# Counting degrees by row over 64 node numbers, scatters behind their piece, four piece buffers, gathers in pairs

## The chip, the core and the metric

The kernel runs on one core of one Trainium2 chip. The metric is the device time of one execution in microseconds, the median of three runs. A profiled execution of the same program gives the trace that all lines below come from. PE is TensorE, ACT is ScalarE, DVE is VectorE, POOL is GpSimd and SP is SyncE.

## The reference, cut to what matters

A graph transformer of two layers over N = 6250 nodes and E = 100000 edges. The edges come sorted by destination. Nodes have one of 16 types, edges one of 32.

```python
def gt_layer(x, ntype, etype, src, dst, Wk, Wq, Wv, Wa, Watt, Wmsg, pri, skip, g, b):
    k = typed_linear(x, ntype, Wk).reshape(n, H, HS)      # and q, v alike
    kT = jnp.einsum('nhd,htdo->nhto', k, Watt)
    vT = jnp.einsum('nhd,htdo->nhto', v, Wmsg)
    kw = kT[src, :, etype]
    m = vT[src, :, etype]
    a = jnp.einsum('ehd,ehd->eh', kw, q[dst]) * pri[:, etype].T / SQRT_D
    att = edge_softmax(a, dst, n)
    msg = (m * att[:, :, None]).reshape(-1, H * HS)
    hag = jax.ops.segment_sum(msg, dst, num_segments=n)
    h = jax.nn.silu(typed_linear(hag, ntype, Wa))
    h = h * alpha + x * (1.0 - alpha)
    return (h - mu) * jax.lax.rsqrt(var + 1e-05) * g + b
```

Two such layers, a last linear layer, and a layer norm over x plus the result. D = 128, H = 8 heads of HS = 16.

## The kernel before

For each layer the kernel first makes a table in HBM, `tabs[l]`: for every node and every edge type the row of 256 numbers kT and vT. The edges of a node then need only gathers: one row of the table per edge. Nodes are sorted by their degree within classes of types, so that the nodes of a block of 128 have nearly the same number of edges; there are NB = 50 such blocks.

The part before the first edge gather, up to `prep.close()`, has these pieces of work:

- **Load and test.** The edges' destinations lie in `dsti`, 128 rows of EC = 782 edges (the last row padded with node number N). L441 to L448 count how often a destination is smaller than the one before. If that is ever so, `tc.If(unsorted > 0)` (L497) sorts the edges by a loop of 782 rounds; otherwise the branch is skipped.
- **Table of layer 0.** Nodes are placed by type (`inv`, `rows1`). For every type t the generator `linears0` (L844) gathers x rows (`xg`, L852), transposes them and makes kT and vT of the type's window. `table_block` (L279) then makes, for each block of 128 nodes, two *pieces* `st` (128 x 4096 f32, 2 MB): for each of the two halves kT and vT of a piece it runs matmuls into PSUM (`tb`, L291) for four pairs of heads and copies them to `st` on ACT (L298), or, for the pairs in `share`, on DVE (L296). It yields after each half. A finished piece goes to HBM by one indirect scatter on POOL (`put0`, L898). `st` has STB0 = 3 buffers. There are 98 pieces.
- **Ranking beside it.** `rank_order` (L566) is a generator whose steps are interleaved with the halves by the loop at L907 to L931. It first runs `degrees` (L450): 46 chunks of 17 edges per row, for each chunk two comparisons on DVE that make one-hot matrices of the destination's low 7 bits (`ol`, L465) and high bits (`oh`, L468), and 17 matmuls (L472) that add them up to the number of edges of each node. Then come the node order (histogram L591 and L600, ranks L696 to L707, and `say`, L735 to L747, which carries node data to rank order as `meta`), and last the rank's gathers: for each of 13 groups of up to four blocks, the edge lists `ell` (L778), the x rows in rank order `xr` (L787), and the store of these rows `xrd` (L790). The yields say "degrees", "gathers", "done", or nothing.
- **The loop.** `stage` is the last word that was yielded. `share` is empty while stage is "" or "degrees", else (1,): one pair of four goes to DVE. After each half the ranking moves on by two steps, in the gathers by one step per piece (on the odd half). A finished piece is kept in `late`; it is scattered when the next piece is made, or later.

POOL's instructions stand in the order in which the program writes them (`manual_schedule`); the other engines' are put in order by a scheduler at build time. After `prep.close()` a load of `over` picks the arm; the `fast` arm runs the edge gathers (L1143) of both layers.

Of the kernel before, what the change touches and what calls it, by code (L numbers as in the profile page):

```python
# [9 lines left out]
F32 = mybir.dt.float32  # L10
BF16 = mybir.dt.bfloat16
I32 = mybir.dt.int32
# [101 lines left out]
def kernel(  # L114
# [44 lines left out]
    STB0 = 3  # L159
# [283 lines left out]
    nfalls = pp.tile([P, 1], F32, name="nfalls")  # L443
    nc.vector.tensor_reduce(nfalls, falls, axis=AX.X, op=ALU.add)
    nf_ps = pps.tile([1, 1], F32, name="ps")
    nc.tensor.matmul(nf_ps, nfalls, ones[:, 0:1], start=True, stop=True)
    nfi = pp.tile([1, 1], I32, name="nfi")
    nc.vector.tensor_copy(nfi, nf_ps)  # L448

    def degrees(got):  # L450

        loi = pp.tile([P, EC], I32, name="loi", tag="lo")
        hii = pp.tile([P, EC], I32, name="hii", tag="srci")
        lob = pp.tile([P, EC], BF16, name="lob")
        hib = pp.tile([P, EC], BF16, name="hib")
        nc.vector.tensor_single_scalar(loi, dsti, P - 1, op=ALU.bitwise_and)
        nc.vector.tensor_single_scalar(hii, dsti, 7, op=ALU.arith_shift_right)
        nc.vector.tensor_copy(lob, loi)
        nc.vector.tensor_copy(hib, hii)
        deg_ps = pps.tile([P, NT], F32, name="ps")  # L460
        for c in range(NCH):
            cols = slice(c * J, (c + 1) * J)
            ol = pp2.tile([P, J, P], BF16, name="ol")
            oh = pp2.tile([P, J, NT], BF16, name="oh")
            nc.vector.tensor_tensor(ol, lob[:, cols].unsqueeze(2).to_broadcast([P, J, P]),  # L465
                                    colb.unsqueeze(1).to_broadcast([P, J, P]), op=ALU.is_equal)
            yield "degrees"
            nc.vector.tensor_tensor(oh, hib[:, cols].unsqueeze(2).to_broadcast([P, J, NT]),  # L468
                                    colb[:, :NT].unsqueeze(1).to_broadcast([P, J, NT]),
                                    op=ALU.is_equal)  # L470
            for j in range(J):
                nc.tensor.matmul(deg_ps, ol[:, j, :], oh[:, j, :],  # L472
                                 start=(c == 0 and j == 0), stop=(c == NCH - 1 and j == J - 1))
            yield "degrees"
        yield
        deg = pp.tile([P, NT], F32, name="deg")
        nc.vector.tensor_copy(deg, deg_ps)
# [14 lines left out]

    unsorted = nc.values_load(nfi[0:1, 0:1], min_val=0, max_val=P * EC)
# [3 lines left out]
    with tc.If(unsorted > 0):  # L497
        found = []
        for _ in degrees(found):
            pass  # L500
# [46 lines left out]
        both = pp.tile([P, EC, 2], I32, name="both")  # L547
# [16 lines left out]
    with tc.manual_schedule(engines={mybir.EngineType.Pool}):  # L564

        def rank_order():  # L566
# [208 lines left out]

            for i0, k in superblocks(NB):
# [7 lines left out]
                yield "gathers"  # L784
# [5 lines left out]
                nc.gpsimd.dma_start(rows(xrd, i0, k), xr[:, :k])  # L790
                yield "gathers"
            yield "done"

            onehot = pp.tile([P, NB, TY], F32, name="onehot", tag="both")
# [760 lines left out]
```

## Time and profile before

| what | us |
|---|---|
| median of three runs (3449.41 to 3453.79) | 3449.84 |
| the profiled execution | 3441.72 |
| its span, first to last instruction | 3439.9 |
| first edge gather (L1143) issued at | 803.08 |
| first piece copied (L298) at, end of the sorted branch (L456) at | 57.38, 42.62 |
| PE, PEld, DVE, ACT, POOL busy over the span | 1804.8, 859.6, 2061.4, 996.2, 2207.3 |
| L1143, 1734 gathers, busy | 1703.1 |
| L898, 98 scatters, busy up to 860 us | 156.2 |

The profile page names an engine, a line of the kernel, the tiles written and read, the number of instructions, the busy time and the mean of one; after it the idle time of the engine just before these instructions, and what ended it. Up to 803 us the waits that matter are those around the pieces:

```profile
POOL tab L898 <- ACT st L298: 223.2, 58, 15.7
ACT st L298 <- PE tb L291: 193.2, 128, 5.5
...
ACT st L298 <- DMA tab<-st,rows: 168.9, 48, 16.0
DVE st L296 <- DMA tab<-st,rows: 150.5, 44, 9.0
```

Each line tells who waited for whom, the total in us, how often, and the longest. A wait of ACT or DVE for "DMA tab<-st,rows" is one for a free buffer: the scatter that reads it has not finished.

### The profile page before, as it was taken

How to read it: one execution, taken by the hardware profiler on the slowest of the kernel's cores; microseconds unless marked ns; L12 is line 12 of the kernel's file. 1: busy time of each engine (PE TensorE's matmuls, PEld its weight loads, DVE VectorE, ACT ScalarE, POOL GpSimd, SP SyncE). 2: the span in 40 equal slices, each digit the busy share in tenths (PEclk: the TensorE clock that was granted, in tenths of full speed). 3: DMA queues.
4: the chain of work that ended last, by engine and by line, in shares of the span. 5: the costliest groups of instructions: out<-in, count | busy, mean ns of one | idle time of the engine just before them, and what ended most of it. 6: DMA issues, size and time to landing. Idle time of an engine off the chain costs nothing. (4 is left out here: it accounts for less than half of the span.)

```text
span 3439.9 us, 24065 instructions
## 1 busy us (share of the span) xinstructions
PE 1804.8 (52%) x6428; PEld 859.6 (25%) x6428; DVE 2061.4 (60%) x4345; ACT 996.2 (29%) x1634; POOL 2207.3 (64%) x2213
## 2 busy tenths in 40 slices
PE   4779776893067667777778777601112122121313
PEld 2445333451022232333233222201001111011111
DVE  8967511223566676667667765346656666566765
ACT  2543333561025223432344246301111111021111
POOL 3741366325767777678777776177767777777773
PEclk9768755666577776877787887655555555555555
DMA  6576476898348656775788488733433333343331
GB/s 173 244 300 272 186 264 261 360 423 246 104 156 282 215 197 233 284 262 196 239 290 294 168 301 324 295 107 114 110 98 109 111 112 106 112 116 110 111 105 50
DMA packets 194493, 691.24 MB, mean 201 GB/s; under 512 B 55469, under 2 KB 106032, under 8 KB 169298
## 3 DMA queue, kind: packets, MB, share of 16 engines
q0 software_dynamic: 119120, 651.15, 53.8%
q1 hardware_dynamic: 58838, 31.29, 3.4%
q10 hardware_dynamic: 16384, 7.11, 1.0%
q8 instruction: 55, 0.90, 0.1%
q14 instruction: 96, 0.79, 0.1%
HBM read 264.91 MB, written 429.48 MB: 202 GB/s over the span
## 5 line engine op out<-in xcount | busy, mean ns | idle before, releaser
L1143 POOL DMA_INDIRECT kv<-tab,ell x1734 | 1703.1, 982 | 573.4 <-issue 460.3
L298 ACT COPY st<-tb 128x512 f32<-128x512 f32 (+1 forms) x1024 | 704.4, 759 | 589.7 <-PE tb L291 335.4
L276 PE MATMUL nb<-ident,hag 128*128 128x128 f32 x100 | 26.1, 399 | 758.4 <-DVE hag L1193 758.4
L1155 DVE TENSOR_TENSOR kv<-kv,tb 128x512 f32<-128x512 f32 (+3 forms) x234 | 150.7, 646 | 379.2 <-DMA kv<-tab,ell 370.5
L1155 DVE TENSOR_TENSOR kv<-kv,q 128x512 f32<-128x512 f32 (+3 forms) x234 | 151.8, 651 | 357.3 <-DMA kv<-tab,ell 346.7
L291 PE MATMUL tb<-bdv,vT 32*128 32x512 f32 x784 | 308.0, 912 | 99.4 <-ACT st L298 97.7
L898 POOL DMA_INDIRECT tab<-st,rows x98 | 156.2, 1594 | 276.6 <-ACT st L298 223.2
L291 PE MATMUL tb<-bdv,kvT 32*128 32x512 f32 x800 | 266.9, 790 | 69.6 <-ACT st L298 69.2
L1159 DVE TENSOR_REDUCE a<-kv 128x32 f32<-128x512 f32 (+3 forms) x468 | 298.2, 640 | 2.2
L296 DVE COPY st<-tb 128x512 f32<-128x512 f32 (+1 forms) x160 | 116.6, 730 | 291.5 <-DMA tab<-st,rows 150.5
L291 PE MATMUL tb<-bdk,kT 32*128 32x512 f32 x784 | 260.2, 938 | 3.3 <-DVE st L296 3.3
L270 PE MATMUL nb<-xm,wa 128*128 128x384 f32 (+1 forms) x384 | 209.7, 708 | 86.6 <-DVE xm L261 86.3
L291 PE MATMUL tb<-bdk,kvT 32*128 32x512 f32 x800 | 241.5, 780 | 19.5 <-ACT st L298 19.0
L1354 POOL DMA_INDIRECT tab<-st,row x100 | 114.8, 1148 | 148.7 <-ACT st L298 104.6
L276 PEld LDWEIGHTS nb<-ident,hag 128*128 128x128 f32 x100 | 15.6, 197 | 778.0 <-issue 560.3
L261 DVE SCALAR_TENSOR_TENSOR xm<-ntb,nb 128x384 f32<-128x384 bf16 (+1 forms) x336 | 185.6, 593 | 38.1 <-PE nb L276 23.7
L270 PE MATMUL nb<-xm,wq 128*128 128x384 f32 (+1 forms) x192 | 100.5, 685 | 139.1 <-DVE xm L261 138.9
L291 PEld LDWEIGHTS tb<-bdv,vT 32*128 32x128 f32 x784 | 107.9, 253 | 189.6 <-ACT st L298 168.5
L1045 ACT COPY tb<-q 128x128 f32<-128x128 f32 x50 | 13.4, 269 | 469.8 <-DVE sums L1088 347.1
L1288 PE MATMUL nb<-xm,wkqv 128*128 128x384 f32 (+1 forms) x288 | 126.3, 590 | 38.4 <-DVE xm L261 28.0
L270 PEld LDWEIGHTS nb<-xm,wa 128*128 128x128 f32 x384 | 94.9, 260 | 200.1 <-DVE xm L261 117.8
L1307 PE MATMUL nb<-xm,wkqv 128*128 128x384 f32 (+1 forms) x288 | 132.5, 619 | 15.1 <-DVE xm L261 14.7
(289 smaller groups left out, 2958.1 us busy)
## 6 DMA issues: line engine op xcount, KB each, us to landing
kv<-tab,ell POOLq DMA_INDIRECT x1734
hr<-xrd SPq DMA_DIRECT2D x30, 192.0 KB, 3.2
hr<-xrd SPq DMA_DIRECT2D x15, 256.0 KB, 4.5
xrd<-xr POOLq DMA_DIRECT2D x11, 256.0 KB
ntb<-typed SPq DMA_DIRECT2D x20, 96.0 KB, 7.2
hrd<-hs SPq DMA_DIRECT2D x10, 192.0 KB, 3.7
qrd<-q SPq DMA_DIRECT2D x10, 192.0 KB, 3.2
q<-qrd SPq DMA_DIRECT2D x10, 192.0 KB, 3.3
```

What stands on the lines that cost most here:

```text
L261: nc.vector.scalar_tensor_tensor(xm[:, :n], ntb[:, :n], float(t), hT[:, :n], op0=ALU.is_equal, op1=ALU.mult)
L270: nc.tensor.matmul(ps[:, :n], w[:, t, :], xm[:, :n], start=(t == types[0]), stop=(t == types[-1]))
L291: nc.tensor.matmul(pt[:, b], yT[s, i * P:(i + 1) * P], bd[s, tt, :], start=True, stop=True)
L296: nc.vector.tensor_copy(to, pt)
L298: nc.scalar.copy(to, pt)
L898: put = nc.gpsimd.indirect_dma_start(out=tabs[0].rearrange("(n t) c -> n (t c)", t=16), out_offset=bass.IndirectOffsetOnAxis(ap=rows1[:, t ...
L1143: get = nc.gpsimd.indirect_dma_start(out=kv[:, j - j0, :], out_offset=None, in_=tabs[l][:], in_offset=bass.IndirectOffsetOnAxis(ap=ell[:, ...
L1155: nc.vector.tensor_tensor(kk, kk, q.unsqueeze(1).to_broadcast([P, c, D]), op=ALU.mult)
L1159: nc.vector.tensor_reduce(a[:, j0:j1, :], kk.rearrange("p k (h d) -> p k h d", h=H), axis=AX.X, op=ALU.add)
L1288: nc.tensor.matmul(outs[j][:, :n], wkqv[:, j, t, :], xm[:, :n], start=(t == types[0]), stop=(t == types[-1]))
L1307: nc.tensor.matmul(ps[:, :n], wkqv[:, j, t, :], xm[:, :n], start=(t == types[0]), stop=(t == types[-1]))
L1354: put = nc.gpsimd.indirect_dma_start(out=tabs[1].rearrange("(n t) c -> n (t c)", t=16), out_offset=bass.IndirectOffsetOnAxis(ap=row2[:, tg ...
```

## The change

Four things are changed in the part before the first edge gather.

1. **Degrees by row.** A row of sorted edges holds few node numbers in succession. The new `degrees` takes the lowest number of each row and counts, for each of the NEAR = 64 numbers from there on, how many of the row's 782 edges have it: one `tensor_scalar` with an accumulated column per number. 16 groups of four numbers then go through one-hot matrices (f32) and a matmul each to the nodes. `nfalls` is also set where a row's numbers span 64 or more; then the branch of L497 is taken, which counts with the old code (now `degrees_any`). The part after the counts is a function of its own, `ordered`. Degrees now yield nothing instead of "degrees", and less often.
2. **Scatters.** `store` issues the scatter at once; `late` is gone. `st` has four buffers. `both`, `lob`, `hib`, `ol` and `oh` of the branch share other tiles' room.
3. **Rank gathers in pairs.** `ell` and `xr` gathers yield after two, and the `xrd` store of a group is issued after the `ell` gathers of the next.
4. **Steps.** One ranking step per half, not two. DVE shares copies in the gathers and after them, and before that in every second block only.

```diff
@@ -156,7 +156,8 @@
     KO = [sum(KB[:b]) for b in range(NB)]
     KS = sum(KB)
     PAD = P * EC + P
-    STB0 = 3
+    STB0 = 4
+    NEAR = 64
     assert D == P and H * HS == D and H == 8 and HS == 16 and EC % J == 0 and NP > N and L == 2
     assert max(KB) * H + P <= 512 and max(KB) <= P and min(KB) >= CH and NR >= NP and NB <= P and TY == NC * TC
 
@@ -440,41 +441,24 @@
     falls = pp.tile([P, EC], F32, name="falls", tag="lo")
     nc.vector.tensor_tensor(falls[:, :EC - 1], dsti[:, :EC - 1], dsti[:, 1:], op=ALU.is_gt)
     nc.vector.tensor_tensor(falls[:, EC - 1:], dsti[:, EC - 1:], nxt, op=ALU.is_gt)
-    nfalls = pp.tile([P, 1], F32, name="nfalls")
-    nc.vector.tensor_reduce(nfalls, falls, axis=AX.X, op=ALU.add)
-    nf_ps = pps.tile([1, 1], F32, name="ps")
-    nc.tensor.matmul(nf_ps, nfalls, ones[:, 0:1], start=True, stop=True)
+    nfalls = pp.tile([P, 2], F32, name="nfalls")
+    nc.vector.tensor_reduce(nfalls[:, 0:1], falls, axis=AX.X, op=ALU.add)
+    lowest = pp.tile([P, 1], F32, name="lowest")
+    nc.vector.tensor_copy(lowest, dsti[:, 0:1])
+    nc.vector.tensor_scalar(nfalls[:, 1:2], dsti[:, EC - 1:], lowest, None, op0=ALU.subtract)
+    nc.vector.tensor_scalar(nfalls[:, 1:2], nfalls[:, 1:2], float(NEAR), None, op0=ALU.is_ge)
+    nc.vector.tensor_tensor(nfalls[:, 0:1], nfalls[:, 0:1], nfalls[:, 1:2], op=ALU.max)
+    nf_ps = pps.tile([P, 1], F32, name="ps")
+    nc.tensor.matmul(nf_ps, ones, nfalls[:, 0:1], start=True, stop=True)
     nfi = pp.tile([1, 1], I32, name="nfi")
-    nc.vector.tensor_copy(nfi, nf_ps)
-
-    def degrees(got):
-
...
-        deg_ps = pps.tile([P, NT], F32, name="ps")
-        for c in range(NCH):
-            cols = slice(c * J, (c + 1) * J)
-            ol = pp2.tile([P, J, P], BF16, name="ol")
-            oh = pp2.tile([P, J, NT], BF16, name="oh")
-            nc.vector.tensor_tensor(ol, lob[:, cols].unsqueeze(2).to_broadcast([P, J, P]),
-                                    colb.unsqueeze(1).to_broadcast([P, J, P]), op=ALU.is_equal)
-            yield "degrees"
-            nc.vector.tensor_tensor(oh, hib[:, cols].unsqueeze(2).to_broadcast([P, J, NT]),
-                                    colb[:, :NT].unsqueeze(1).to_broadcast([P, J, NT]),
-                                    op=ALU.is_equal)
-            for j in range(J):
-                nc.tensor.matmul(deg_ps, ol[:, j, :], oh[:, j, :],
-                                 start=(c == 0 and j == 0), stop=(c == NCH - 1 and j == J - 1))
-            yield "degrees"
-        yield
-        deg = pp.tile([P, NT], F32, name="deg")
-        nc.vector.tensor_copy(deg, deg_ps)
+    nc.vector.tensor_copy(nfi, nf_ps[0:1, :])
+    far = pp.tile([P, 1], F32, name="far")
+    nc.vector.tensor_scalar(far, nf_ps, 1.0, None, op0=ALU.min)
+    deg_far = pp.tile([P, NT], F32, name="deg_far")
+    nc.vector.memset(deg_far, 0.0)
+
+    def ordered(got, deg):
+
         tot_ps = pps.tile([P, NT], F32, name="ps")
         nc.tensor.matmul(tot_ps, ones, deg, start=True, stop=True)
         tot = pp.tile([P, NT], F32, name="tot")
@@ -490,13 +474,81 @@
         got.append((deg, ptr))
         yield
 
+    def degrees_any(got):
...
+        nc.vector.tensor_copy(deg_far, deg_ps)
+        yield from ordered(got, deg_far)
+
+    def degrees(got):
+
+        rel = pp.tile([P, EC], F32, name="rel", tag="lo")
+        nc.vector.tensor_scalar(rel, dsti, lowest, None, op0=ALU.subtract)
+        nid = pp.tile([P, NEAR], I32, name="nid")
+        nc.vector.tensor_scalar(nid, colf[:, :NEAR], lowest, None, op0=ALU.add)
+        parts = pp.tile([P, 2, NEAR], I32, name="nidparts")
+        nc.vector.tensor_single_scalar(parts[:, 0], nid, P - 1, op=ALU.bitwise_and)
+        nc.vector.tensor_single_scalar(parts[:, 1], nid, 7, op=ALU.arith_shift_right)
+        at = pp.tile([P, 2, NEAR], F32, name="nidat")
+        nc.vector.tensor_copy(at, parts)
+        yield
+        near = pp.tile([P, NEAR], F32, name="near")
+        same = pp.tile([P, EC], BF16, name="same_dst", tag="eti")
+        deg_ps = pps.tile([P, NT], F32, name="ps")
+        for c0 in range(0, NEAR, SB):
+            for c in range(c0, c0 + SB):
+                nc.vector.tensor_scalar(same, rel, float(c), None, op0=ALU.is_equal, op1=ALU.add,
+                                        accum_out=near[:, c:c + 1])
+            yield
+            sl = slice(c0, c0 + SB)
+            ol = pp2.tile([P, SB, P], F32, name="oc")
+            nc.vector.tensor_tensor(ol, at[:, 0, sl].unsqueeze(2).to_broadcast([P, SB, P]),
+                                    colf.unsqueeze(1).to_broadcast([P, SB, P]), op=ALU.is_equal)
+            oh = pp2.tile([P, SB, NT], F32, name="rh", bufs=1)
+            nc.vector.tensor_tensor(oh, at[:, 1, sl].unsqueeze(2).to_broadcast([P, SB, NT]),
+                                    colf[:, :NT].unsqueeze(1).to_broadcast([P, SB, NT]),
+                                    op=ALU.is_equal)
+            nc.vector.tensor_tensor(oh, oh, near[:, sl].unsqueeze(2).to_broadcast([P, SB, NT]),
+                                    op=ALU.mult)
+            for c in range(c0, c0 + SB):
+                nc.tensor.matmul(deg_ps, ol[:, c - c0, :], oh[:, c - c0, :],
+                                 start=(c == 0), stop=(c == NEAR - 1))
+            if c0 % 8:
+                yield
+        yield
+        deg = pp.tile([P, NT], F32, name="deg")
+        nc.vector.tensor_copy(deg, deg_ps)
+        nc.vector.tensor_tensor(deg_far, deg_far, deg, op=ALU.subtract)
+        nc.vector.scalar_tensor_tensor(deg, deg_far, far, deg, op0=ALU.mult, op1=ALU.add)
+        yield from ordered(got, deg)
+
     unsorted = nc.values_load(nfi[0:1, 0:1], min_val=0, max_val=P * EC)
 
     cnt = dram.tile([NP + P, 1], I32, name="cnt")
     order = dram.tile([P * EC, 2], I32, name="order")
     with tc.If(unsorted > 0):
         found = []
-        for _ in degrees(found):
+        for _ in degrees_any(found):
             pass
         ptr = found[0][1]
         ptri = pp.tile([P, NT], I32, name="ptri")
@@ -544,7 +596,7 @@
             nc.gpsimd.indirect_dma_start(
                 out=order[:], out_offset=bass.IndirectOffsetOnAxis(ap=pos[:, 0:1], axis=0),
                 in_=pair, in_offset=None)
-        both = pp.tile([P, EC, 2], I32, name="both")
+        both = tp.tile([P, EC, 2], I32, name="both", tag="st", bufs=STB0)
         nc.sync.dma_start(both, order.rearrange("(p j) c -> p j c", p=P))
         nc.vector.tensor_copy(dsti, both[:, :, 0])
         nc.vector.tensor_copy(kvi, both[:, :, 1])
@@ -773,6 +825,7 @@
             nc.sync.dma_start(typed, tyr)
             yield "gathers"
 
+            stored = []
             for i0, k in superblocks(NB):
                 for b in range(i0, i0 + k):
                     nc.gpsimd.indirect_dma_start(
@@ -781,17 +834,22 @@
 
                     nc.vector.tensor_scalar(neg[:, KO[b]:KO[b] + KB[b]], colf[:, :KB[b]],
                                             degr[:, b:b + 1], -BIG, op0=ALU.is_ge, op1=ALU.mult)
-                yield "gathers"
+                    if (b - i0) % 2 or b == i0 + k - 1:
+                        yield "gathers"
+                if stored:
+                    nc.gpsimd.dma_start(*stored.pop())
                 xr = tp.tile([P, SB, D], F32, name="xr")
                 for i in range(k):
                     nc.gpsimd.indirect_dma_start(
                         out=xr[:, i, :], out_offset=None, in_=x,
                         in_offset=bass.IndirectOffsetOnAxis(ap=some[:, i0 + i:i0 + i + 1], axis=0))
-                nc.gpsimd.dma_start(rows(xrd, i0, k), xr[:, :k])
-                yield "gathers"
+                    if i % 2 or i == k - 1:
+                        yield "gathers"
+                stored.append((rows(xrd, i0, k), xr[:, :k]))
+            nc.gpsimd.dma_start(*stored.pop())
             yield "done"
 
-            onehot = pp.tile([P, NB, TY], F32, name="onehot", tag="both")
+            onehot = pp.tile([P, NB, TY], F32, name="onehot")
             nc.vector.tensor_tensor(onehot, meta[:, 3].unsqueeze(2).to_broadcast([P, NB, TY]),
                                     colf[:, :TY].unsqueeze(1).to_broadcast([P, NB, TY]),
                                     op=ALU.is_equal)
@@ -904,7 +962,7 @@
                 tc.declare_no_dep(put.ins, other.ins, reason="rows of other nodes")
             tables0.append(put)
 
-        got, stage, late = [], "", []
+        got, stage = [], ""
         for _ in linears0(got, 0):
             pass
         for t in range(TY):
@@ -912,21 +970,14 @@
             beside = linears0(got, t + 1) if t + 1 < TY else iter(())
             for b in range(b0, b1):
                 def store(tg, st, b=b):
-                    late.append((st, tg, b))
-                share = () if stage in ("", "degrees") else (1,)
+                    put0(st, tg, b)
+                share = (1,) if stage in ("gathers", "done") or (not stage and b % 2) else ()
                 for half, _ in enumerate(table_block(tp, tnb, *got[t], b - b0, share, STB0, store)):
                     next(beside, None)
-                    if half % 2 and len(late) > 1:
-                        put0(*late.pop(0))
-
                     if stage != "gathers" or half % 2:
-                        stage = next(ranking, None)
-                    if stage != "gathers":
-                        stage = next(ranking, None)
+                        stage = next(ranking, "done")
             for _ in beside:
                 pass
-        while late:
-            put0(*late.pop(0))
         for _ in ranking:
             pass
```

More of the change, by code (lines that the diff above doesn't have):

```diff
@@ L442 @@
     nc.vector.tensor_tensor(falls[:, EC - 1:], dsti[:, EC - 1:], nxt, op=ALU.is_gt)
-    nfalls = pp.tile([P, 1], F32, name="nfalls")
-    nc.vector.tensor_reduce(nfalls, falls, axis=AX.X, op=ALU.add)
-    nf_ps = pps.tile([1, 1], F32, name="ps")
-    nc.tensor.matmul(nf_ps, nfalls, ones[:, 0:1], start=True, stop=True)
-    nfi = pp.tile([1, 1], I32, name="nfi")
-    nc.vector.tensor_copy(nfi, nf_ps)
-    def degrees(got):
[L452 to L459, printed above, removed]
-        deg_ps = pps.tile([P, NT], F32, name="ps")
-        for c in range(NCH):
-            cols = slice(c * J, (c + 1) * J)
-            ol = pp2.tile([P, J, P], BF16, name="ol")
-            oh = pp2.tile([P, J, NT], BF16, name="oh")
-            nc.vector.tensor_tensor(ol, lob[:, cols].unsqueeze(2).to_broadcast([P, J, P]),
-                                    colb.unsqueeze(1).to_broadcast([P, J, P]), op=ALU.is_equal)
-            yield "degrees"
-            nc.vector.tensor_tensor(oh, hib[:, cols].unsqueeze(2).to_broadcast([P, J, NT]),
-                                    colb[:, :NT].unsqueeze(1).to_broadcast([P, J, NT]),
-                                    op=ALU.is_equal)
-            for j in range(J):
-                nc.tensor.matmul(deg_ps, ol[:, j, :], oh[:, j, :],
-                                 start=(c == 0 and j == 0), stop=(c == NCH - 1 and j == J - 1))
-            yield "degrees"
-        yield
-        deg = pp.tile([P, NT], F32, name="deg")
-        nc.vector.tensor_copy(deg, deg_ps)
@@ L491, in degrees @@
         yield
+    def degrees_any(got):
+        loi = pp.tile([P, EC], I32, name="loi", tag="lo")
+        hii = pp.tile([P, EC], I32, name="hii", tag="srci")
+        lob = pp.tile([P, EC], BF16, name="lob", tag="eti")
+        hib = pp.tile([P, EC], BF16, name="hib", tag="onehot")
+        nc.vector.tensor_single_scalar(loi, dsti, P - 1, op=ALU.bitwise_and)
+        nc.vector.tensor_single_scalar(hii, dsti, 7, op=ALU.arith_shift_right)
+        nc.vector.tensor_copy(lob, loi)
+        nc.vector.tensor_copy(hib, hii)
+        deg_ps = pps.tile([P, NT], F32, name="ps")
+        for c in range(NCH):
+            cols = slice(c * J, (c + 1) * J)
+            ol = tp.tile([P, J, P], BF16, name="ol", tag="st", bufs=STB0)
+            oh = tp.tile([P, J, NT], BF16, name="oh", tag="st", bufs=STB0)
+            nc.vector.tensor_tensor(ol, lob[:, cols].unsqueeze(2).to_broadcast([P, J, P]),
+                                    colb.unsqueeze(1).to_broadcast([P, J, P]), op=ALU.is_equal)
+            nc.vector.tensor_tensor(oh, hib[:, cols].unsqueeze(2).to_broadcast([P, J, NT]),
+                                    colb[:, :NT].unsqueeze(1).to_broadcast([P, J, NT]),
+                                    op=ALU.is_equal)
+            for j in range(J):
+                nc.tensor.matmul(deg_ps, ol[:, j, :], oh[:, j, :],
+                                 start=(c == 0 and j == 0), stop=(c == NCH - 1 and j == J - 1))
+        nc.vector.tensor_copy(deg_far, deg_ps)
+        yield from ordered(got, deg_far)
@@ new lines, in degrees @@
+    def degrees(got):
[11 more added lines that the diff above has]
+        same = pp.tile([P, EC], BF16, name="same_dst", tag="eti")
+        deg_ps = pps.tile([P, NT], F32, name="ps")
+        for c0 in range(0, NEAR, SB):
[10 more added lines that the diff above has]
+                                    colf[:, :NT].unsqueeze(1).to_broadcast([P, SB, NT]),
+                                    op=ALU.is_equal)
+            nc.vector.tensor_tensor(oh, oh, near[:, sl].unsqueeze(2).to_broadcast([P, SB, NT]),
[11 more added lines that the diff above has]
+        yield from ordered(got, deg)
```

## The prediction

> **What bounds the kernel now.** The page's 40 slices come first: until about 800 us the table of layer 0 is made, then two rounds of edge gathers follow. The chain of waits is short (its last pieces are L1387 scatters at 3431 us), so I read the stage that the diff touches by stretches. I cut it where the timeline changes its work: degrees (to 227 us, where deg is copied), rank (to 380, where meta is copied), gathers (to 620, after the last xrd store), pieces alone (to 790), landing (to 803.08, the first gather of L1143).
>
> ```profile
> core 0: us, PE busy (x) PEld busy (x) DVE busy (x) ACT busy (x) POOL busy (x), PEclk, DMA share, GB/s
> 57.00:227.00 170.00, 129.76 (x1177) 67.75 (x1173) 152.06 (x136) 97.36 (x192) 109.32 (x46) 0.71 0.64 264
> 227.00:380.00 153.00, 138.84 (x692) 86.27 (x690) 104.15 (x205) 55.22 (x106) 24.63 (x27) 0.81 0.58 238
> 380.00:620.00 240.00, 168.95 (x475) 82.82 (x470) 58.82 (x149) 89.16 (x172) 151.15 (x164) 0.56 0.68 252
> 620.00:790.00 170.00, 154.58 (x529) 81.36 (x523) 49.90 (x77) 103.14 (x199) 40.31 (x44) 0.68 0.99 414
> 790.00:803.00 13.00, 0.00 (x0) 0.00 (x0) 0.97 (x2) 0.30 (x1) 0.27 (x1) 0.50 0.99 362
> ```
>
> The DMA share is the column to see: 0.99 only once nothing but pieces is left. Before that the engines are kept waiting, by VectorE (152 of 170 us), by PE and VectorE in turn, and by something that no share shows. The same stretches for the scatter line alone:
>
> ```profile
> 57.00:227.00 170.00, 80.28 (x22) 0.71 0.64 264
> 227.00:380.00 153.00, 16.05 (x16) 0.81 0.58 238
> 380.00:620.00 240.00, 26.56 (x26) 0.56 0.68 252
> 620.00:790.00 170.00, 33.05 (x34) 0.68 0.99 414
> ```
>
> So 98 scatters leave at 7.7, 9.6, 9.2 and 5.0 us each. The last, at a full DMA, is the floor: 170 x 0.99 / 34 = 4.95 us. VectorE's groups up to 860 us, then GpSimd's timeline, tell why the others are slow:
>
> ```profile
> L465 DVE TENSOR_TENSOR ol<-lob,colb 128x2176 bf16<-128x2176 bf16 x46 | 111.5, 2424 | 18.0 <-PE ps L472 17.1 <-PEq L497 0.9
> L468 DVE TENSOR_TENSOR oh<-hib,colb 128x833 bf16<-128x833 bf16 x46 | 47.1, 1024 | 0.0
> ```
> ```profile
> 152.46 24.05 POOL L898 DMA_INDIRECT tab<-st,rows  x1 [3.22 <-ACT st L298]
> ...
> 411.65 0.94 POOL L787 DMA_INDIRECT xr<-in_x_dram,some  x1 [0.30 <-issue]
> 415.56 0.80 POOL L790 DMA_DIRECT2D xrd<-xr  x1 [2.96 <-DMA xr<-in_x_dram,some]
> 416.67 1.04 POOL L898 DMA_INDIRECT tab<-st,rows  x1 [0.30 <-issue]
> ```
>
> Degrees are 158.6 us of VectorE. In the gather stage GpSimd is never free: four L778, a scatter, four L787, a 3 us wait of the L790 store for its rows, the store and a scatter make 16.6 us for two pieces (400.05 to 416.67). Meanwhile ACT, VectorE and PE wait for st buffers.
>
> **The change, stage by stage.** On each engine the two built programs have the same order of instructions from the load of `over` on, so the time from the first L1143 to the end stays. Only 803 us can move.
>
> *Degrees.* Removed: 46 x (2.424 + 1.024) = 158.6 us of VectorE, four casts of 0.56, and 782 matmuls (33.9 us). Added, near branch: 64 counts (128x782 f32, with an accumulated column), 16 groups of one 512-wide and two 196-wide tensor operations, and 64 f32 matmuls of 49 columns. No row shows a count that accumulates. Two rows of that size bound it:
>
> ```profile
> 7.96 0.97 DVE L444 TENSOR_REDUCE nfalls<-falls 128x1 f32<-128x782 f32 x1
> 42.62 0.57 DVE L456 TENSOR_SCALAR loi<-dsti 128x782 int32<-128x782 int32 x1 [1.03 <-DVEq L497]
> ```
>
> L456 is the operation without its sum, L444 the sum. I take 0.97, because a running sum must pass every element, plus 0.06 (the smallest VectorE row, L555) to hand the sum out: 64 x 1.03 = 66 us. From below 64 x 0.57 = 36. From above the scan of 784 at L379, 1.78: 114. A group costs 0.66 (L735) + 2 x 0.35 (L739) = 1.36.
>
> By the Trainium skill, "VectorE: DVE Perf Modes", section on the perf-mode tier table, fp32 tensor_scalar in SBUF runs at two elements a cycle, which fits L456; it does not say whether an accumulated output keeps that. By it alone the counts would take the 36 us above.
>
> The VectorE order of the new program puts 11 groups, four shared copies and a few table copies ahead of the last count: 42.6 (start of L456) + 0.6 for the four new tiny instructions before the branch + 66 + 15 + 8 = 132 us. The first odd block has then passed; six pieces are out. The degrees now take 25 steps, one per half piece, so 12.5 pieces, against 92 steps, two per half. The seven pieces left go at some 5 us: the stage ends at 132 + 35 = 167 with 13 pieces out. From below 137, from above 215. The matmuls hide: 64 pairs at the L600 rate (98 in 20.3 us) are 13 us of PE over 110.
>
> *Rank, 65 steps.* Two steps per half become one, so the same work is spread over 32 pieces, not 16. Each part by its own limit:
> - About 12 halves of small chains: 6 pieces at 5.3 = 32 us.
> - 13 histogram steps: PE needs 1.8 (L600 x8 at half clock) + 2.09 (one half of a piece): 3.9 x 13 = 51.
> - 26 rank halves, 13 pieces: VectorE per piece 5 x 0.66 + 0.69 (half of the pieces share two copies) + 0.5 for table copies = 4.5; PE 1.8 + 2 x 1.14 + 0.8 = 4.9; DMA 4.95. I take 5.3: 69.
> - 13 `say` steps: rl has one buffer, so L735, L743 and L747 follow each other, 0.66 + 0.98 + 1.62 = 3.3, as now (340 to 380 us). The half piece fits beside: 43.
>
> Sum 195 us: 167 to 362, 45 pieces out. At the DMA's floor it would be 32 x 4.95 = 160.
>
> *Gathers, 53 pieces.* Two gathers per piece instead of four, and a store is issued after the next ell gathers, so its 40.9 us of waits (L790) fall away; the rows will have landed before, since two or three scatters stand between. GpSimd: 53 x 1.31 + 100 x 1.25 + 13 x 1.1 + 18 xg x 1.25 + 4 of memsets = 235 us, 4.4 per piece. DMA: 53 x 4.95 = 262, and the gathers and stores, which now take 0.68 x 240 - 26 x 4.95 = 34.5: 297, at 0.99 300 us. So the DMA becomes the bound, 5.7 per piece, and this includes the landing. Steps after "done" run on VectorE from meta on, ahead of the last copies; they cost nothing while VectorE is a third busy, and 8 us if they fell behind.
>
> Immediate scatters and a fourth buffer have no price of their own: four buffers let ACT wait less (now 168.9 us for scatters), but none of that beats 4.95.
>
> The first L1143 comes at 362 + 300 + 1.3 (801.74 to 803.08) = 664, not 803: 139 us less. The profiled execution, 3441.72 us with 1.8 around its 3439.9 span, would be 3303. The median shown is 8.1 higher; the same 139 off 3449.84 gives 3311, so **3310 us**.
>
> One more row counts against the change: beside the degrees' L465, which has two SBUF inputs, scatters took 3.6 us (80.28 / 22), beside the rank's f32 operations 1.0 (16.05 / 16). The Trainium skill, "GPSIMD Engine Reference", section "Specifications", says that GpSimd shares its SBUF interfaces with VectorE and contends with instructions in a two-port mode or with two SBUF inputs. The rank's operations have two such inputs too, so the trace agrees only in part. If the counts run two-port, the rule expects them to hold GpSimd up as well; it names no price.
>
> **The rivals.**
> - *The DMA keeps pace throughout.* For it: a fourth buffer, and the DMA share of 0.64 and 0.58 is all that is lost. DMA work by the table is 0.64 x 170 + 0.58 x 153 + 0.68 x 240 + 0.99 x 183 = 542; 57 + 542 / 0.99 = 605, 198 less: 3252. Against it: 66 us of counts before the sixth piece. 0.14.
> - *The chain of the rank's steps is the bound, not their number per half.* If a half with one step costs what one with two costs now (153 / 33 = 4.6), the stage takes 65 x 4.6 = 301, not 195: 33 us less, 3417. For it: L735 waits 15.0 us for L747, L600 runs at half clock. Against: rank steps are held by VectorE, whose load per half is halved. 0.13.
> - *Scatters starve beside the counts: slower.* A scatter took 24.05 us (152 to 176) while VectorE ran without a gap; it ended as VectorE fell idle. If all 13 did, the stage would end at 57 + 13 x 24 = 369: 202 later, net 63 slower, 3513. It decides from 19 us per scatter ((167 - 57 + 139) / 13). Against: the mean was 3.6 with more VectorE work. 0.06.
> - *The near count is never used.* Were any row to span 64 nodes, the branch with 782 rounds of three indirect transfers would run, at over 1.2 us each 2,800 us more: 6250. A row holds 782 edges at 16 a node, some 49 nodes. 0.01.
>
> **The numbers.** Forecast 0.66, within 3258 (counts at 0.57, half of the rank's loss gone) and 3385 (counts at 1.78, rank partly chained). The range of 8 in 10 reaches down to the first rival, 3250, and up to 3385; the second's upper part, the third and fourth stay out. A change of 0.2% is what a measurement here can tell. Faster 0.92 (the first three cases with 3310, 3252 and 3417, less a little of the last), same 0.02, slower 0.06.
>
> **What would show it.** Right: count rows of about 1.0 us; 13 scatters by some 165 us, 45 by some 360; GpSimd's waits at the store gone; DMA share over 0.95 in the gather stage; the first L1143 near 664; rows from there on as before. Wrong: DMA share under 0.85 while gathers run (GpSimd or PE still bounds); scatter rows of many microseconds beside the counts; rank halves at over 4 us; or later gathers that take longer than 2637 us in all (3439.9 - 803).

## The result, and the profile after

The changed kernel takes 3345.55 us (median of four executions, 3337.76 to 3350.42) against 3451.11 (3449.41 to 3453.79): ratio 0.9691, 95% interval 0.9670 to 0.9713. That is 105.6 us less, where 139 were forecast, and it lies within the range.

One landmark splits the profiled execution (3350.42 us, span 3348.6) cleanly: the first edge gather of layer 0, line L1194 now, L1143 before. It starts at 704.46 us, not at 803.08, and not at the forecast 664. What follows it takes 2644.1 us, against 2636.8. So the stage before the landmark is 98.6 us shorter, of 139 forecast; the other 7 us of the 105.6 lie within the spread of the executions.

The stages of the table, cut where the pieces' counts change: up to the 13th scatter, to the 45th, to the last, and the landing. Columns are the stretch, its length, each engine's busy time, the granted clock, the DMA share and GB/s.

```profile
core 0: us, PE busy (x) PEld busy (x) DVE busy (x) ACT busy (x) POOL busy (x), PEclk, DMA share, GB/s
57.00:168.00 111.00, 86.77 (x356) 44.67 (x352) 82.54 (x218) 49.23 (x96) 20.84 (x23) 0.66 0.56 231
168.00:379.00 211.00, 198.69 (x960) 110.91 (x955) 116.61 (x251) 120.57 (x236) 53.07 (x59) 0.81 0.78 324
379.00:690.00 311.00, 250.08 (x889) 125.83 (x886) 92.85 (x174) 170.62 (x335) 183.64 (x197) 0.74 0.97 385
690.00:704.00 14.00, 0.00 (x0) 0.00 (x0) 0.43 (x2) 0.00 (x0) 0.76 (x1) 0.50 0.75 286
```

Multiply each length by its DMA share and add: 62 + 165 + 302 + 10 = 539 us of transfers. The same product for the kernel before was 542 (the first rival's sum). So the transfers stayed as they were, within the rounding of the shares. The change took idle time of the DMA away: 746 - 542 = 204 us before, 647 - 539 = 108 us now. The sum holds in every experiment below: from 57 us to the first gather, length times DMA share is 534 to 541 us in all twelve, so up to there they differ in how long the DMA stands idle and hardly in what it moves.

The counts in the trace, VectorE's groups from 57 to 168 us (busy us, mean ns of one after the bar):

```profile
L520 DVE TENSOR_SCALAR_CACHE_REDUCE same_dst<-rel 128x782 bf16<-128x782 f32 x55 | 53.1, 965 | 1.0
L520 DVE DVE_READ_ACCUMULATOR same_dst<-rel 128x1 f32 x55 | 4.5, 82 | 0.0
```

A count is two instructions, 0.97 and 0.08 us: 1.05, where 1.03 was taken. The place where time was lost against the forecast shows in GpSimd's timeline and, below it, TensorE's, in the gather stage:

```profile
414.00 1.17 POOL L956 DMA_INDIRECT tab<-st,rows  x1 [0.30 <-issue]
...
418.88 1.02 POOL L956 DMA_INDIRECT tab<-st,rows  x1 [0.30 <-ACT st L299]
420.20 0.98 POOL L910 DMA_INDIRECT xg<-in_x_dram,inv  x1 [0.31 <-PE tb L292]
421.49 0.94 POOL L910 DMA_INDIRECT xg<-in_x_dram,inv  x1 [0.30 <-PE tb L292]
422.74 0.94 POOL L910 DMA_INDIRECT xg<-in_x_dram,inv  x1 [0.30 <-issue]
```
```profile
419.82 1.44 PE L292 MATMUL tb<-bdv,vT 32*128 32x512 f32 x3
431.33 0.69 PE L932 MATMUL l<-ident,xg 128*128 128x128 f32 x2 [10.08 <-DMA xg<-in_x_dram,inv]
```

The `xg` gathers (the x rows of the next type) leave right behind two piece scatters. TensorE, which works in order, waits 10.08 us for their rows. No piece is made meanwhile: the next scatters go at 427.11 and 437.34, and the DMA share from 367 to 520 us is 0.91:

```profile
367.00:520.00 153.00, 122.28 (x460) 57.47 (x453) 56.34 (x142) 84.46 (x166) 87.97 (x95) 0.79 0.91 365
```

### The profile page after: what moved, and what is told of

Its sections match the earlier page's. It is cut to its first block, busy times and chain, and to the rows that moved or that the text cites. A ratio compares the mean times of both kernels' runs of the same rounds, so it can differ in the third digit from the quotient of the medians.

```text
span 3348.6 us, 22789 instructions
## 1 busy us (share of the span) xinstructions
PE 1756.3 (52%) x5774; PEld 827.5 (25%) x5774; DVE 1991.3 (59%) x4438; ACT 992.9 (30%) x1634; POOL 2141.0 (64%) x2213
## 5 line engine op out<-in xcount | busy, mean ns | idle before, releaser
L1194 POOL DMA_INDIRECT kv<-tab,ell x1734 | 1709.4, 986 | 577.1 <-issue 463.9
L956 POOL DMA_INDIRECT tab<-st,rows x98 | 102.3, 1044 | 295.1 <-ACT st L299 243.7
L292 PE MATMUL tb<-bdv,vT 32*128 32x512 f32 x784 | 249.1, 799 | 25.4 <-ACT st L299 18.1
L292 PE MATMUL tb<-bdk,kT 32*128 32x512 f32 x784 | 237.8, 793 | 0.0
L292 PEld LDWEIGHTS tb<-bdv,kvT 32*128 32x128 f32 x800 | 76.1, 224 | 182.1 <-ACT st L299 140.1
## 6 DMA issues: line engine op xcount, KB each, us to landing
xrd<-xr POOLq DMA_DIRECT2D x11, 256.0 KB, 12.7
```

What stands on the lines that cost most here:

```text
L292: nc.tensor.matmul(pt[:, b], yT[s, i * P:(i + 1) * P], bd[s, tt, :], start=True, stop=True)
L956: put = nc.gpsimd.indirect_dma_start(out=tabs[0].rearrange("(n t) c -> n (t c)", t=16), out_offset=bass.IndirectOffsetOnAxis(ap=rows1[:, t ...
L1194: get = nc.gpsimd.indirect_dma_start(out=kv[:, j - j0, :], out_offset=None, in_=tabs[l][:], in_offset=bass.IndirectOffsetOnAxis(ap=ell[:, ...
```

## The experiments

All twelve, with the kernel before timed on the same chip in each group. "First gather" is the start of the first edge gather in the profiled execution, "behind it" the rest of that span.

| Kernel | us, median | ratio to before (95%) | first gather | behind it |
|---|---|---|---|---|
| changed kernel | 3345.55 | 0.9691 (0.9670 to 0.9713) | 704.46 | 2644.1 |
| e1 counts alone | 3438.68 | 0.9980 (0.9964 to 0.9997) | 801.00 | 2638.3 |
| e2 two steps | 3375.87 | 0.9792 (0.9757 to 0.9827) | 735.93 | 2637.9 |
| e3 three buffers | 3352.88 | 0.9715 (0.9679 to 0.9751) | 708.93 | 2643.6 |
| e4 four gathers | 3409.87 | 0.9885 (0.9851 to 0.9920) | 767.19 | 2647.7 |
| e5 late scatters | 3743.67 | 0.9663 (0.9600 to 0.9726) | 678.54 | 3063.2 |
| e6 last store behind | 3777.27 | 0.9725 (0.9662 to 0.9789) | 707.42 | 3087.8 |
| e7 counts apart | 3789.34 | 0.9769 (0.9710 to 0.9828) | 731.95 | 3070.8 |
| e8 counts in bf16 | 3798.53 | 0.9807 (0.9742 to 0.9872) | 710.07 | 3060.7 |
| e9 xg sooner | 3330.96 | 0.9643 (0.9622 to 0.9664) | 685.32 | 2650.3 |
| e10 late again | 3320.96 | 0.9618 (0.9594 to 0.9642) | 679.11 | 2640.0 |
| e11 late, xg sooner | 3327.53 | 0.9638 (0.9617 to 0.9659) | 677.01 | 2631.6 |
| e12 three steps a group | 3322.94 | 0.9627 (0.9602 to 0.9652) | 688.93 | 2638.8 |

e5 to e8 ran on a chip where the kernel before took 3889.38 us, some 440 more, and the kernel of e5 423 more than in e10. In the traces all of it lies behind the first gather. These four are read by the first gather, not by their totals.

**e1: the degrees alone.** The changed kernel with its other parts undone.

```diff
-    STB0 = 4
+    STB0 = 3
...
-                    if (b - i0) % 2 or b == i0 + k - 1:
-                        yield "gathers"
...
+                yield "gathers"
...
-                    put0(st, tg, b)
-                share = (1,) if stage in ("gathers", "done") or (not stage and b % 2) else ()
+                    late.append((st, tg, b))
+                share = () if stage in ("", "degrees") else (1,)
...
+                    if half % 2 and len(late) > 1:
+                        put0(*late.pop(0))
...
+                    if stage not in ("gathers", "done"):
                         stage = next(ranking, "done")
```

> Only the degrees are new: three buffers, scatters a piece late, two ranking steps per half piece and one step for four gathers, as in the kernel before. Theory of the prediction (only DMA time counts, and a shorter stage also takes fewer pieces): the degrees' 25 steps now pass beside 6 pieces instead of 22 and end near 137 us, rank 153 us with 16 pieces, gathers 240 us with 26, and the 50 pieces left go alone at 5.0: 137 + 153 + 240 + 248 + 13 = 791, so about 12 us less than before, 3438. Rival (the degrees are the gain, the rest follows at its old pace): the 95 us that the stage is shorter come off nearly whole, 3365.

3438.68 us; first gather 801.00, 2 us earlier than before. Its windows, cut where `deg` is copied, at the first ell gather, behind the last store, and at the last scatter:

```profile
core 0: us, PE busy (x) PEld busy (x) DVE busy (x) ACT busy (x) POOL busy (x), PEclk, DMA share, GB/s
57.00:132.00 75.00, 63.71 (x229) 36.52 (x228) 69.86 (x196) 28.21 (x56) 10.60 (x12) 0.56 0.41 170
132.00:289.00 157.00, 141.90 (x677) 87.47 (x677) 103.28 (x209) 54.28 (x103) 27.23 (x31) 0.78 0.49 203
289.00:525.00 236.00, 169.51 (x479) 84.72 (x480) 58.51 (x147) 90.55 (x174) 147.30 (x159) 0.56 0.70 266
525.00:789.00 264.00, 245.09 (x813) 125.67 (x807) 78.25 (x121) 158.67 (x304) 68.14 (x77) 0.66 0.96 399
```

The degrees end at 132 us, 95 earlier than before, and nothing comes of it: 22 pieces, not 38, have left when the ell gathers begin, and the rest is made up at the end, 51 pieces alone in 264 us. With the landing (12 us at a share of 1.00) the sum again is 538 us of transfers. The rival (95 us off) falls.

**e2: two ranking steps per half again, outside the gathers.**

```diff
                     if stage != "gathers" or half % 2:
                         stage = next(ranking, "done")
+                    if stage not in ("gathers", "done"):
+                        stage = next(ranking, "done")
```

> The changed kernel with two ranking steps per half piece outside the gathers again. Theory: degrees to 137 with 6 pieces, rank in 153 with 16, gathers at 5.9 per piece with 53, and 23 pieces left alone at 5.0: first gather of layer 0 near 730 instead of 704, so about 25 us slower than the changed kernel, 3370. Rival (the rank is bound by the chain of its steps, their number per half does not matter): rank shorter and pieces caught up, within 4 us of the changed kernel.

First gather 735.93, 31.5 us later; total 3375.87. The ell gathers begin at 294.14 instead of 379.90, but with 23 pieces out, not 45. The theory said 730 and 3370. So the number of steps per half does matter, and "the chain of the rank's steps is the bound" falls.

**e3: three buffers.** `STB0 = 3` in place of 4, nothing else.

> The changed kernel with three piece buffers. Theory of the prediction: the fourth buffer has no price of its own, within 4 us of the changed kernel, 3345. Rival: the buffers carry the DMA over the halves that wait for VectorE and over the small gathers; with three, ACT waits for scatters (now 42.8 us in the gather stage) and the DMA share there falls under 0.95: 10 to 30 us slower, 3355 to 3375.

First gather 708.93, 4.5 us later, just over the theory's bound of 4 us. The ratio's interval covers the ratio of the changed kernel, so the total doesn't tell them apart. The rival named the right sign, since the DMA share from 379 to 690 us is 0.94 and not 0.97, but its 10 to 30 us are not there.

**e4: the gathers as before.**

```diff
-                    if (b - i0) % 2 or b == i0 + k - 1:
-                        yield "gathers"
-                if stored:
-                    nc.gpsimd.dma_start(*stored.pop())
+                yield "gathers"
...
-                    if i % 2 or i == k - 1:
-                        yield "gathers"
-                stored.append((rows(xrd, i0, k), xr[:, :k]))
-            nc.gpsimd.dma_start(*stored.pop())
+                nc.gpsimd.dma_start(rows(xrd, i0, k), xr[:, :k])
+                yield "gathers"
```

> The changed kernel with the gathers as before: four per step, and the store right behind its gathers. Theory: 26 pieces beside the gathers in about 240 us, GpSimd waiting about 3 us at each of 13 stores, then 27 pieces alone at 5.0: 378 + 240 + 135 + 13 = 766, 60 us slower than the changed kernel, 3405. Rival (with four buffers and immediate scatters the DMA stays full anyway): within 10 us, 3355.

First gather 767.19, 62.7 us later, total 3409.87: the largest single part. The window of its gather stage, and from its GpSimd waits the line of the store:

```profile
380.00:620.00 240.00, 172.28 (x493) 83.32 (x495) 55.86 (x118) 95.39 (x183) 153.07 (x167) 0.59 0.70 264
```
```profile
POOL xrd L842 <- DMA xr<-in_x_dram,some: 35.3, 11, 4.7
```

The DMA share falls from 0.97 to 0.70 even with four buffers and immediate scatters, and the store's waits are back (35.3 us at 11 stores).

**e5: late scatters, otherwise the changed kernel.**

```diff
-                    put0(st, tg, b)
+                    late.append((st, tg, b))
...
                     next(beside, None)
+                    if half % 2 and len(late) > 1:
+                        put0(*late.pop(0))
```

> The changed kernel with each piece's scatter issued a piece late again. Theory of the prediction: the immediate scatter has no price of its own; the DMA holds three other pieces, first gather of layer 0 within 5 us of 704, total within 5 us of the changed kernel, 3346. Rival: with four buffers one is now always filled and not on its way, as if there were three, and in the degree and rank stages, where the DMA runs dry, each piece starts some 5 us later: 5 to 20 us slower, 3351 to 3366.

Both theories missed, on the same side: the first gather comes at 678.54, 26 us *earlier*. The immediate scatter does have a price.

**e6: the last rows' store behind the last piece.**

```diff
-            nc.gpsimd.dma_start(*stored.pop())
+            last.append(stored.pop())
             yield "done"
...
         for _ in ranking:
             pass
+        nc.gpsimd.dma_start(*last.pop())
```

> The changed kernel with the last xrd store issued behind the last piece's scatter. Theory: the store's 9.7 us wait held back the last scatter (678.9 to 689.8 us), but the DMA had other pieces under way for most of it; from 670 to 705 us it was idle for 0.12 x 35 = 4 us, so the first gather of layer 0 comes about 4 us earlier, near 700. Rival A: the whole wait comes off, 694. Rival B: the store itself now lands last, behind the piece, 704 or later.

GpSimd's timeline at the end of the stage, first the changed kernel, then this one:

```profile
688.64 0.80 POOL L849 DMA_DIRECT2D xrd<-xr  x1 [9.71 <-DMA xr<-in_x_dram,some]
689.75 1.01 POOL L956 DMA_INDIRECT tab<-st,rows  x1 [0.30 <-issue]
704.46 0.99 POOL L1194 DMA_INDIRECT kv<-tab,ell  x1 [13.70 <-SPq L1602]
```
```profile
685.82 1.00 POOL L957 DMA_INDIRECT tab<-st,rows  x1 [2.05 <-DMA tab<-st,rows]
693.67 0.81 POOL L984 DMA_DIRECT2D xrd<-xr  x1 [6.86 <-DMA xr<-in_x_dram,some]
707.42 1.00 POOL L1196 DMA_INDIRECT kv<-tab,ell  x1 [12.94 <-SPq L1604]
```

The last scatter leaves 4 us sooner, and the store now ends the stage: no gain (rival B). The 9.71 us wait, GpSimd's only long one at a store, is worth nothing: the last scatter and the last store both have to land, and the DMA share from 670 to 705 us is 1.00 here.

**e7: all counts ahead of all groups,** two counts a step, no copies on VectorE beside them, one step for four ell gathers.

```diff
+        for c in range(NEAR):
+            nc.vector.tensor_scalar(same, rel, float(c), None, op0=ALU.is_equal, op1=ALU.add,
+                                    accum_out=near[:, c:c + 1])
+            if c % 2 == 1:
+                yield "counts"
         for c0 in range(0, NEAR, SB):
-            for c in range(c0, c0 + SB):
-                nc.vector.tensor_scalar(same, rel, float(c), None, op0=ALU.is_equal, op1=ALU.add,
-                                        accum_out=near[:, c:c + 1])
-            yield
...
-                    if (b - i0) % 2 or b == i0 + k - 1:
+                    if (b - i0) % 4 == 3 or b == i0 + k - 1:
...
-                share = (1,) if stage in ("gathers", "done") or (not stage and b % 2) else ()
+                share = (1,) if stage in ("gathers", "done") or (stage is None and b % 2) else ()
```

> The changed kernel with all 64 counts ahead of the 16 groups, a step for every two counts (32 steps), no copies on VectorE beside the counts, and one step for four ell gathers. Theory: in the degree stage TensorE stands still for rh in its order (44 us of waits at the matmuls of the counts), and the pieces behind these matmuls with it; with the matmuls behind all counts, 22 pieces pass beside the degrees at about 5.5 us each, which end near 181 us; against 13 pieces at 168 that is 35 us less, first gather of layer 0 near 669, total near 3310. Rival A (VectorE's counts, not TensorE's order, hold the pieces, through a shared port or the buffers): 12 us per piece stays, stage ends near 320 us with 22 pieces, no gain, 3345 or more. Rival B (TensorE at half clock bounds): pieces at 7 us, the stage ends at 211, 5 us less, 3340.

First gather 731.95, 27 us later: a miss. Windows beside the counts, then beside the groups:

```profile
57.00:157.00 100.00, 77.74 (x281) 39.19 (x281) 59.81 (x167) 67.05 (x136) 23.26 (x27) 0.78 0.74 306
157.00:228.00 71.00, 68.58 (x214) 39.64 (x211) 22.60 (x53) 20.19 (x39) 8.78 (x11) 0.53 0.41 170
```

The first half is near what the theory said: with the matmuls out of the way pieces leave at some 6.4 us (16 from 60.5 to 156.4), not 5.5, and the DMA share is 0.74 instead of 0.56. But the 16 groups' matmuls then come in a clump, two groups per half piece, and TensorE, busy 68.58 of 71 us at a granted clock of 0.53, lets four pieces through in 65 us (162.33 to 227.42). Rival A is out, rival B named the right engine in the second half. How much of the 27 us comes from there is not shown: the step of four ell gathers was changed too, and the DMA share behind 442 us, up to the last scatter, is 0.92 where the changed kernel has 0.97 in its gather stage.

**e8: the counted numbers in bf16.** `rel` as BF16.

> The changed kernel with the node numbers that are counted held as bf16 (128x782 bf16 read, bf16 written). Theory: a count with an accumulated column passes one element a cycle whatever the type, 0.97 us as now, total within 5 us of the changed kernel, 3346. Rival: the type sets the pace and the count takes 0.3 to 0.57 us: the counts end 26 to 43 us earlier, total 20 to 35 us less, 3311 to 3326.

VectorE's timeline of this kernel:

```profile
62.38 0.97 DVE L520 TENSOR_SCALAR_CACHE_REDUCE same_dst<-rel 128x782 bf16<-128x782 bf16 x1
63.27 0.08 DVE L520 DVE_READ_ACCUMULATOR same_dst<-rel 128x1 f32 x1
```

Same 0.97 us; first gather 710.07, no gain. The Trainium skill, "VectorE: DVE Perf Modes", section "The DVE is not a fixed-function vector unit", says that a faster mode is taken only where a micro-op program for it exists; the two equal rows fit an accumulating count that has none.

**e9: scatters at once, the transposes of xg three half pieces later.**

```diff
             at = nc.values_load(shift_t[0:1, t:t + 1], ...)
             yield
+            for _ in range(3):
+                yield
```

> The changed kernel, scatters still at once, but the transposes of xg come three half pieces later, so the four xg gathers have some 9 us more to land. Theory (an immediate scatter makes GpSimd wait for ScalarE in its order, the xg gathers behind it are issued late and then land behind scatters, and TensorE, in order too, stands still: 85.3 us of waits for xg between 57 and 700 us): these waits fall under 35 us, the DMA share from 367 to 520 us rises from 0.92 to over 0.97, and the first gather of layer 0 comes near 685 instead of 704, total near 3326. Rival (what the late scatter gained is GpSimd's own time or the buffer order, not xg): 704 and 3346 as in the changed kernel.

685.32, where the theory said 685; total 3330.96. The transposes' matmuls on TensorE and the time that it sat idle ahead of them for `xg` (us, times), in the changed kernel, in e9, and in e10:

```profile
L932 PE MATMUL l<-ident,xg x45: 272/421/476, 60.3 to 607.9; 128*128 128x128 f32 x45
  DMA xg<-in_x_dram,inv: 36.5, 11
```
```profile
L934 PE MATMUL l<-ident,xg x45: 272/421/476, 78.1 to 588.4; 128*128 128x128 f32 x45
  DMA xg<-in_x_dram,inv: 14.7, 5
```
```profile
L932 PE MATMUL l<-ident,xg x45: 272/421/475, 62.3 to 576.0; 128*128 128x128 f32 x45
  DMA xg<-in_x_dram,inv: 5.9, 3
```

Waits and first gather go together: 22 us less of waits for 19 us, 31 less for 25. The 85.3 us in the expectation adds the idle time of the weight loads (48.8) to that of the matmuls (36.5), which overlap; these sums are 85.3, 35.0 and 15.8, the same picture. The DMA share from 367 to 520 us rises to 0.98, as the theory said:

```profile
367.00:520.00 153.00, 127.93 (x480) 64.02 (x479) 57.41 (x126) 93.42 (x182) 98.36 (x106) 0.75 0.98 391
```

**e10: late scatters once more,** the kernel of e5.

> The same kernel as e5 once more, since there every time lay some 440 us higher, that of the kernel before too, outside the stage under study. Theory: first gather of layer 0 near 679 and 26 us less than the changed kernel, 3320, ratio to the kernel before 0.962. Rival (the first gather came early by chance): 704, 3346, ratio 0.969.

679.11 and 3320.96 us, ratio 0.9618 (0.9594 to 0.9642), against 0.9691 (0.9670 to 0.9713) of the changed kernel. It beats both kernels. The xg gathers of the type shown above, in its GpSimd timeline:

```profile
396.00 0.94 POOL L910 DMA_INDIRECT xg<-in_x_dram,inv  x1 [0.30 <-PE tb L292]
397.25 0.94 POOL L910 DMA_INDIRECT xg<-in_x_dram,inv  x1 [0.30 <-DMA ell<-kvs,start]
398.49 0.94 POOL L910 DMA_INDIRECT xg<-in_x_dram,inv  x1 [0.30 <-issue]
...
400.23 1.02 POOL L956 DMA_INDIRECT tab<-st,rows  x1 [0.17 <-issue]
...
404.48 1.21 POOL L956 DMA_INDIRECT tab<-st,rows  x1 [0.30 <-ACT hT L934]
```

They are now issued at 396, not 420, behind the 50th scatter and not the 52nd. Its windows, cut at the 13th scatter, the first ell gather (358.85; the 45th scatter, a piece late, goes at 366.72), the last scatter and the first edge gather:

```profile
57.00:162.00 105.00, 83.44 (x361) 43.16 (x356) 83.27 (x221) 50.31 (x98) 21.17 (x24) 0.71 0.56 232
162.00:359.00 197.00, 191.97 (x941) 107.04 (x938) 112.01 (x220) 115.79 (x227) 53.66 (x59) 0.82 0.83 343
359.00:660.00 301.00, 261.94 (x905) 125.87 (x903) 97.90 (x205) 176.29 (x344) 182.39 (x196) 0.72 0.99 397
660.00:679.00 19.00, 0.00 (x0) 0.00 (x0) 0.78 (x2) 0.00 (x0) 1.05 (x2) 0.50 0.89 340
```

537 us of transfers, 85 idle: 46 beside the degrees, 34 beside the rank, 5 in the rest.

**e11: both remedies.** The edits of e9 and e10 together.

> Late scatters and the xg transposes three half pieces later together. Theory: both take away the same wait; with late scatters 17.8 us of it were left and the DMA share from 367 us on was already 1.00, so only some 3 to 8 us more come off in the degrees and the rank: first gather near 673, total 3314. Rival (they are separate gains): 20 us more, 3300.

677.01, another 2 us; the total (3327.53) is not apart from e10's. In e11 TensorE no longer waits for xg at all between 57 and 700 us. They take away the same wait, as the theory said; its 3 to 8 us were a little high.

**e12: three steps per group of four counts,** on top of e11, and one step for four ell gathers.

```diff
                                         accum_out=near[:, c:c + 1])
-            yield
+                if c % 2:
+                    yield
...
-            if c0 % 8:
-                yield
+            yield
...
-                    if (b - i0) % 2 or b == i0 + k - 1:
+                    if (b - i0) % 4 == 3 or b == i0 + k - 1:
```

> As e11, and the degrees in three steps per group of four counts (two counts, two counts, the group) instead of one and a half, with one step for four ell gathers. Some 28 pieces then pass beside the degrees. Theory: the degree stage's DMA share of 0.56 comes from the steps, each half piece waiting for one; with more half pieces than VectorE's steps, TensorE sets the pace, 6.1 us a piece at half clock: degrees end near 229 us with 28 pieces, 15 more than at 161, which is 7 us better than e11: first gather near 666, total 3307; at full clock 5 us a piece, 643 and 3284. Rival (a piece beside counts takes 8 us or more whatever the steps): degrees end past 280 us, 40 us slower than e11.

First gather 688.93, 12 us later than e11; total 3322.94, not apart from it. The windows up to the end of the degrees, of the rank, of the gathers:

```profile
57.00:224.00 167.00, 148.23 (x550) 75.45 (x549) 97.02 (x245) 92.78 (x180) 39.57 (x45) 0.66 0.72 298
224.00:427.00 203.00, 197.96 (x958) 108.71 (x955) 112.82 (x222) 118.78 (x233) 54.34 (x59) 0.83 0.80 334
427.00:665.00 238.00, 201.03 (x698) 103.38 (x700) 77.10 (x173) 135.34 (x263) 161.34 (x172) 0.70 0.96 381
```

The degrees end at 224 us (229 was worked out), but with 24 scatters out, not some 28: a piece takes some 7 us, not 6.1. The DMA share beside them is 0.72 instead of 0.56, over a longer stage, so that its idle time stays: 47 + 41 + 10 us. TensorE is busy 148 of 167 and 198 of 203 us in the first two stages, at a clock of 0.66 and 0.83, which points to it as what sets their pace. What would keep its clock up was not tried.

## Why the prediction was right, and where its size was off

The forecast was 57 us, plus 520 us of transfers (98 x 4.95 + 34.5), plus 87 us in which the DMA waits: 664. Measured: 57 + 539 + 108 = 704.

- **Degrees: the sum right, in part by luck.** 167 us with 13 pieces forecast, the 13th scatter at 168.09. The count was 1.05 us, not 0.57. But the last count ended at 121.8 us, not 132 (seven groups stood ahead of it, not eleven), and the seven pieces behind it took 46 us, not 35; the two errors cancel. "The matmuls hide" was counted too low: the 98 rows of L600 are single matmuls, so 64 pairs at that rate are 26.5 us, not 13, and from 57 to 168 us they took 24.3. From 122 to 168 us TensorE was busy 40.23 of 46 us. No scatter starved: 12 took 13.02 us from 57 to 168 us, 1.09 each, the six beside the counts 0.98 to 1.44, so the third rival is out. The rule of the Trainium skill's "GPSIMD Engine Reference", section "Specifications", that was weighed there doesn't show beside the counts, which read one SBUF tensor.
- **Rank: one wait left out, one term too small.** 362 forecast for the 45th scatter, 378.62 measured. From the 13th scatter to the 45th it took 210.5 us, not 195. With the xg waits gone there it is 203 to 205 (e9, e10, e11), so they are worth 6 to 7 of the 16 us. The rest lies mostly in the 26 rank halves: forecast 69 us, taken 85 (first L754 at 242.28 to the last L759 at 327.37; 75 to 82 in e9 to e11). The sum gave TensorE 4.9 us a piece there; it was busy some 6, at a clock of 0.94, and hardly idle:

```profile
250.00:331.00 81.00, 76.30 (x406) 43.34 (x405) 50.75 (x90) 47.70 (x94) 21.02 (x24) 0.94 0.79 327
```

No run changed TensorE's work there; that it sets the pace is read from this row and was not tried.

- **"Immediate scatters and a fourth buffer have no price of their own": half wrong.** The buffer is worth 4.5 us (e3). The immediate scatter costs 25 us: 704.46 against 679.11. It is the one step that failed outright. I looked for what the piece itself gains, and not for what stands behind the scatter on GpSimd: the xg gathers, whose late landing holds TensorE. They were counted only as 18 x 1.25 us of GpSimd's time.
- **Gathers: the mechanism right, the term too small.** The DMA is the bound (0.97; 0.99 in e10). From the 45th scatter to the first edge gather it took 325.8 us, not 300. "This includes the landing" was wrong. In e10 the last 53 pieces are issued in 294 us, close to the 300, and 18.75 us of landing come on top. The prediction's own numbers would have shown it: the forecast's 520 us of transfers stood 22 below the 542 in the rival's sum. Stretch by stretch these are the 12.9 us of the landing (0.99 x 13) and 0.58 x 153 - 16 x 4.95 = 9.5 us beside the rank.
- **The store's waits: right, save the last.** 40.9 us went, one wait of 9.71 was left at the last store, and it was worth nothing (e6).
- **"The time from the first L1143 to the end stays": right within its spread.** 2644.1 against 2636.8; eight other programs with that same part, on chips of the same pace, span 2631.6 to 2650.3.
- **The rivals.** The DMA does not keep pace beside degrees and rank (0.56, 0.78); the chain is not the bound (the rank took 210 us, not 301, and e2); the near count is used.

By undoing one part at a time, the parts are worth, at the first gather: pairs of gathers 62.7 us, one step per half 31.5, the fourth buffer 4.5, late scatters in place of immediate ones 25.4 the other way. The degrees alone are worth 2 us (e1). These do not add up to the 98.6 us, since each part's worth depends on the others. That the new degrees pay only beside the other parts is argued and not shown: no run kept the old degrees with the other three parts, so what they add there is not known.

## What to carry to other kernels

Where a shared queue bounds a stage, add up length x share for each stretch: if the transfers' time is the same after an edit, only the idle part can move, and a forecast whose transfers add up to less than the measured ones has left something out, most likely the landing. Before an instruction is moved forward in an in-order queue, look at what stands behind it and who waits for that: small loads that an engine needs soon belong ahead of large stores that nobody waits for. A faster stage is worth only what the bounding resource can do with the time.

## What the hardware showed that was not expected

- An accumulating count over 782 numbers takes 0.97 us whether these are f32 or bf16, and 0.08 us more for reading the sum.
- Small gathers issued among scatters of 2 MB land late: the xg gathers of the changed kernel took 2.5 us to land up to the first scatter (0 to 60 us) and 4.3 to 11.7 us from 57 to 700 us. From the issue of the first of them at 420.20 to the transposes at 431.33 some 11 us passed, and the xrd store took 12.7 us (median) from issue to landing.
- The same program took 423 us longer on one chip, all of it behind the first edge gather; the table's stage kept its time (e5 678.54, e10 679.11). The cause was not looked into.
